# Experts that add their rows to per-token sums in DRAM, and logits taken from the narrow projection

## The chip, the cores and the metric

One core of a Trainium2 chip runs the whole kernel in one launch. The metric is device microseconds (us) from start to end, smaller is better. The engines are named as in the profile: PE (TensorE, matmuls), PEld (its weight loads), DVE (VectorE), ACT (ScalarE), POOL (GpSimd), SP (SyncE). SP, ACT and POOL each issue DMAs from a queue of their own. All numbers are float32.

## The reference, cut to what matters

```python
xn = layernorm(x)                                 # x: 8 sequences, 512 tokens, D = 256
out = x + attn(xn) * silu(ffn(xn))

def attn(x):                                      # 16 heads of 16
    q, k, v = silu(x @ Wq), l2_norm(silu(x @ Wk)), x @ Wv
    gk = log_sigmoid(x @ Wf1 @ Wf2)               # decay, by key
    a = k * -sigmoid(x @ Wgamma) * exp(gk)
    for t in range(512):                          # S: 16 x 16 for each head
        S = S * exp(gk[t])
        S = S + k[t] * (a[t] @ S + v[t])
        o[t] = q[t] @ S
    o = o * sigmoid(x @ Wog1 @ Wog2)
    return layernorm(o) * norm_w @ Wo

def ffn(x):                                       # 8 experts, each token takes 2
    w = softmax(x @ Wg + bg)
    top_w, top = top_k(w, 2);  cw = top_w / sum(top_w)
    out = sum(cw[e] * (gelu(x @ W1[e] + b1[e]) @ W2[e] + b2[e]) for e in top)
    return layernorm(out) * gamma + beta
```

## The kernel before

**Tiling.** The 4096 tokens are cut into eight stretches of 64 steps of all eight sequences (512 tokens, 4 tiles of 128 rows, `NP = 4`, `NT = 32` in all). Each stretch has four chunks of 16 steps, so the recurrence is a chain of 32 chunks.

**Prologue.** `load_tokens` loads x, half by SP's queue and half by ACT's. For every stretch `norm` normalizes in place, `transposed` (L208) turns the rows on PE, `logits` (L217) makes the gate's logits with 16 matmul records into the PSUM bank `pg`. Then `project(0)` runs: a narrow projection with `wfg_sb` (Wf1, Wgamma and Wog1 side by side, 80 columns), from which the decay is made with Wf2 (L258), then keys and queries (L231, L267) and values (L274). Results pass through the three buffers `stage` to DRAM; `spread` (L241) writes `kqd`. `gate` (L444 to L486) picks each token's two experts and their shares; inside it `route` (L300 to L431) counts the tokens of each expert, gives each of the 8192 token copies a row in `xs_dram` (`slot`), rounds the experts' ranges up to tiles of 256 rows (39 tiles, `NX`), finds the rows that stay free and the expert of each tile (`owner`). `scatter` (L493) writes the rows there: 64 indirect DMAs for two copies of 32 tiles, 14 with zeros for the free rows.

**Recurrence.** DVE prepares each stretch (`fine` and `solve`, L567 to L676). `fetch` and `turn_keys` (L515 to L529) load `kqd` and the gate g and turn them. Each chunk then takes `by_state` (L758, PE, which reads the state S), `sdec` (L767, POOL: S times its decay), `add_v` (L791, DVE, writes RO; POOL stores it to `ro`), `by_keys` (L825, PE) and `renew` (L837, DVE: the new S from PSUM and `sdec`). `output` (L888, L897, DVE) adds the part of the output inside a chunk; `attend` (L1032 to L1088) normalizes and projects a stretch and stores it in `att`.

**Experts.** `experts` runs over 39 tiles. SP loads the tile's rows (L933) and, at the address read from `owner` (L924), its expert's weights (L926, L928). PE makes h (L966), ACT applies gelu (L974). For each half n of a tile PE adds b2, picked by the one-hot `owned` (L986), and h times W2 (L994) in one PSUM bank; ACT copies both halves (L1004) and POOL stores them to `y_dram` (L950), in the order of `xs_dram`.

**Finish.** `gather` (L1098) fetches for each token tile its two rows of `y_dram` by `slot`: 64 indirect DMAs on POOL. `finish` scales one on ACT (L1113), adds the other with its share on DVE (L1117), normalizes, applies gamma, beta and silu, multiplies by `att` (L1146), adds x (L1148), which SP loads again (L1144), and stores (L1150, POOL).

**Order.** Every engine works through its instructions in a fixed order. The program is written out by three queues of generators, `inner` (recurrence's preparation), `between` (attention) and `beside` (everything else), which `stretch` spends credit on between the steps of the chain; a compile-time scheduler may move an instruction forward in front of others on its engine. `per_chunk` is the credit that `beside` gets in each chunk: projections of seven stretches and 39 expert tiles are spread over `PART` = 0.85 of the chunks.

## Time and profile before

| | |
|---|---|
| median of 9 runs | 1309.08 us (1292.92 to 1359.27) |
| profiled execution | 1306.15 us, its span 1304.4 us |
| mean granted PE clock | 0.852 |
| busy: PE, DVE, ACT, POOL | 979.4, 1070.3, 501.5, 413.0 us |
| DMA | 230.20 MB, mean 176 GB/s |
| renewals of the state (L837) | first at 236.6 us, last at 1196.1 us |
| last store to y_dram (L950) issued | 1054.8 us |

The profile comes from one execution. A busy engine isn't always the bound: what counts is which wait ends last in each stage, so the stages are read one by one: prologue (0 to 60), start of the chain with the projections (60 to 332), chain and experts together (332 to 1055), and the end (1055 to 1304).

### The profile page before, as it was taken

Reading aid. Unit: us, or ns where it says so; the run is one execution under the profiler, and the core shown is the slowest. Engines: PE = TensorE matmul, PEld = TensorE weight load, DVE = VectorE, ACT = ScalarE, POOL = GpSimd, SP = SyncE. Lnnn points to the kernel's source line nnn. Section 1 sums busy time; section 2 is a strip of 40 time slices with the busy share of each in tenths; the row PEclk is TensorE's granted clock in tenths of the full one; section 3 lists DMA queues with packets and bytes.
Section 4 is the critical chain, followed back from the end, with each engine's and each line's share of the span. In section 5 each row is a group of like instructions: output and inputs, shape, how many; then the busy total and the mean of one; then the engine's idle time right before and its main releaser. Section 6 shows DMA issues by size and latency. Waiting matters only on the chain.

```text
span 1304.4 us, 20560 instructions
## 1 busy us (share of the span) xinstructions
PE 979.4 (75%) x7679; PEld 738.4 (57%) x7679; DVE 1070.3 (82%) x2050; ACT 501.5 (38%) x814; POOL 413.0 (32%) x275
## 2 busy tenths in 40 slices
PE   5987657859999979999999899899998951310022
PEld 4743323438878768877787688678876830210021
DVE  5479675996999999999999998999999722768742
ACT  1375225435334234443442453344343212435222
POOL 0037781024115402511421141015111547782000
PEclk9998776879999979999999899889998975655566
DMA  8068575669768977796899589657947783463532
GB/s 173 1 175 205 154 225 108 158 184 280 216 191 257 152 193 241 232 204 167 264 167 250 150 283 213 168 166 259 205 133 218 141 172 114 126 187 86 97 80 64
DMA packets 389730, 230.20 MB, mean 176 GB/s; under 512 B 280024, under 2 KB 355904, under 8 KB 388608
## 3 DMA queue, kind: packets, MB, share of 16 engines
q1 hardware_dynamic: 368176, 176.99, 56.4%
q0 software_dynamic: 14672, 45.63, 11.2%
q10 hardware_dynamic: 6784, 6.29, 2.0%
q8 instruction: 60, 0.98, 0.3%
q14 instruction: 38, 0.31, 0.1%
HBM read 157.29 MB, written 71.57 MB: 175 GB/s over the span
## 4 chain that ended last, share of the span: by engine, by line
DVE 45%; DMA 14%; PE 13%; issue 11%; SPq 6%; ACT 5%; POOL 4%; ACTq 1%; DVEq 0%; POOLq 0%
DMA o<-O 5%; DVE Z L676 5%; DVE scratch_a L668 5%; DVE O L897 4%; DVE scratch_o L888 4%; DVE scratch_q L593 4%; DVE Z L610 4%; PE pp L231 3%; DVE scratch_a L593 3%; DVE Z L606 3%; DVE A L606 3%; DVE S L837 2%; POOL y L1098 2%; SPq L924 2%; PE pg L217 2%
## 5 line engine op out<-in xcount | busy, mean ns | idle before, releaser
L994 PE MATMUL py<-w,h 128*128 128x256 f32 x1248 | 307.0, 401 | 9.2 <-ACT h L974 9.2
L966 PE MATMUL ph<-xT_s,w 128*128 128x256 f32 x1248 | 289.5, 387 | 15.9 <-ACT sg L1057 7.2
L767 POOL TENSOR_TENSOR sdec<-S,PcF 128x1024 f32<-128x1024 f32 x31 | 181.6, 5858 | 367.1 <-DVE S L837 282.5
L994 PEld LDWEIGHTS py<-w,h 128*128 128x128 f32 x1248 | 240.7, 198 | 71.4 <-issue 24.8
L966 PEld LDWEIGHTS ph<-xT_s,w 128*128 128x128 f32 x1248 | 236.9, 193 | 52.5 <-ACT sg L1057 7.6
L974 ACT ACTIVATE h<-ph,bias 128x256 f32<-128x256 f32 x312 | 129.2, 473 | 116.3 <-PE ph L966 116.1
L668 DVE TENSOR_TENSOR scratch_a<-Z,A 128x1020 f32<-128x1020 f32 (+29 forms) x120 | 97.2, 810 | 15.5 <-ACT fq L632 15.4
L493 POOL DMA_INDIRECT xs_dram<-xn,slot x64 | 78.4, 1225 | 99.5 <-DVE which L406 80.3
L676 DVE TENSOR_TENSOR Z<-Z,scratch_a 128x1020 f32<-128x1020 f32 (+29 forms) x120 | 99.5, 830 | 0.2
L1004 ACT COPY y<-py 128x512 f32<-128x512 f32 x39 | 22.8, 584 | 185.7 <-PE py L994 185.7
L593 DVE TENSOR_TENSOR scratch_q<-Z,X 128x64 f32<-128x64 f32 (+15 forms) x128 | 93.3, 729 | 0.0
L606 DVE TENSOR_REDUCE Z<-scratch_q 128x4 f32<-128x64 f32 (+15 forms) x128 | 91.0, 711 | 0.0
L610 DVE TENSOR_TENSOR Z<-Z,X 128x64 f32<-128x64 f32 (+14 forms) x120 | 85.5, 712 | 0.0
L593 DVE TENSOR_TENSOR scratch_a<-Z,X 128x64 f32<-128x64 f32 (+14 forms) x120 | 84.6, 705 | 0.0
L606 DVE TENSOR_REDUCE A<-scratch_a 128x4 f32<-128x64 f32 (+14 forms) x120 | 81.0, 675 | 0.0
L950 POOL DMA_DIRECT2D y_dram<-y x39 | 28.7, 736 | 160.8 <-ACT y L1004 146.5
L1074 PE MATMUL pz<-ident,o_f 128*128 128x128 f32 x64 | 13.7, 340 | 85.9 <-ACT o_f L1028 71.0
L888 DVE TENSOR_TENSOR scratch_o<-Z,R 128x192 f32<-128x192 f32 (+22 forms) x120 | 72.4, 604 | 1.2 <-ACT fq L632 1.2
L897 DVE TENSOR_TENSOR O<-O,scratch_o 128x192 f32<-128x192 f32 (+22 forms) x120 | 73.0, 608 | 0.0
L825 PE MATMUL PC<-RO,KT 16*64 16x64 f32 x1984 | 34.6, 239 | 47.2 <-issue 22.2
L758 PE MATMUL PC<-S,FA 64*32 64x64 f32 x2048 | 31.5, 237 | 44.8 <-DVE S L837 41.1
L825 PEld LDWEIGHTS PC<-RO,KT 16*64 16x64 f32 x1984 | 28.1, 138 | 59.1 <-issue 27.5
(193 smaller groups left out, 1499.9 us busy)
## 6 DMA issues: line engine op xcount, KB each, us to landing
w<-in_L_ffn_W_dram SPq DMA_DIRECT2D x78, 1024.0 KB
kqd<-st_p SPq DMA_DIRECT2D x48, 256.0 KB
raw<-kqd SPq DMA_DIRECT2D x8, 1536.0 KB
xs<-xs_dram SPq DMA_DIRECT2D x39, 256.0 KB
y_dram<-y POOLq DMA_DIRECT2D x39, 256.0 KB
fq<-fq SPq DMA_DIRECT2D x8, 1024.0 KB
ro<-RO POOLq DMA_DIRECT2D x16, 512.0 KB
KT<-kt SPq DMA_DIRECT2D x132, 32.0 KB
```

The source lines that it names most:

```text
L493: ins = nc.gpsimd.indirect_dma_start(out=xs_dram[:, :], out_offset=bass.IndirectOffsetOnAxis(ap=to, axis=0), in_=what, in_offset=None,)
L593: nc.vector.tensor_tensor(pr, Z[:, :, :upto, C:], step[:, m, i].unsqueeze(2).to_broadcast([P, n, upto, HD]), ALU.mult,)
L606: nc.vector.tensor_reduce(to, pr, AX.X, ALU.add)
L610: nc.vector.tensor_tensor(Z[:, :, :i, C:], Z[:, :, :i, C:], step[:, 2, i].unsqueeze(2).to_broadcast([P, n, i, HD]), ALU.mult,)
L668: nc.vector.tensor_tensor(pr, Z[:, :, l, l:].unsqueeze(2).to_broadcast([P, n, l, w]), A[:, :, l, :l].unsqueeze(3).to_broadcast([P, n, l, w ...
L676: nc.vector.tensor_tensor(Z[:, :, :l, l:], Z[:, :, :l, l:], kept.pop(l), ALU.add)
L767: nc.gpsimd.tensor_tensor(dec.rearrange(flat), S.rearrange(flat), PcF[:, :, c].unsqueeze(2).to_broadcast([P, 16, SB]), ALU.mult,)
L888: nc.vector.tensor_tensor(pr, Z[:, :, j, j:C].unsqueeze(3).to_broadcast(shape), R[:, j].unsqueeze(2).to_broadcast(shape), ALU.mult,)
L897: nc.vector.tensor_tensor(o, o, kept.pop(j), ALU.add)
L966: nc.tensor.matmul(ph[:, k], w1[:, j, (f + k) * P : (f + k + 1) * P], xT[:, j], start=(j == 0), stop=(j == KD - 1),)
L974: nc.scalar.activation(h[:, k], ph[:, k], AF.Gelu, bias=bias[:, t, f + k : f + k + 1])
L994: nc.tensor.matmul(py[:, n], hs[f // 2][:, f % 2, n * P : (n + 1) * P], w2[:, f], start=False, stop=(f == NF - 1),)
```

## The change

1. **Sums in DRAM.** A scattered row becomes 258 wide: behind the 256 values stand the token's number and the share of that copy (`rows`, `DX`). `experts` scales each half tile by the share on ACT while it leaves PSUM, and an indirect DMA on POOL adds it to the token's row of `y_dram` (`add_to_sums`); rows of free places go to 128 spare rows. `start_sums` writes the shares' mix of b2 there first, so that the experts' bias matmuls go. In place of `gather`, `fetch_sums` loads whole tiles from SP.
2. **Logits.** `wfg_sb` gets Wg as columns 96 to 103; `narrow` runs this projection for every stretch in the prologue, transposes the logits back, and stores f1, og and the raw g in DRAM from ACT's queue. `project` loads f1 and makes the decay after keys and queries; g's sigmoid moves to `turn_keys`.
3. **x by the store.** SP copies x to out, DRAM to DRAM, and the last store adds to it.
4. Smaller: every other stretch's first half of x is loaded by POOL's queue, the weights of the narrow projection before them; `vz` is cleared by POOL at the start; `att_f` has three buffers, `xs` four; `per_chunk` reckons 12.8 for a projection, not 15.3.

```diff
...
-    xs_dram = dram.tile([NX * TS, D], F32, name="xs_dram")
-    y_dram = dram.tile([NX * TS, D], F32, name="y_dram")
+    DX = D + 2
+    xs_dram = dram.tile([NX * TS, DX], F32, name="xs_dram")
+    y_dram = dram.tile([NT * P + P, D], F32, name="y_dram")
...
+    rows = tokens.tile([P, NT, DX], F32, name="rows")
+    xn = rows[:, :, :D]
+    nc.gpsimd.iota(rows[:, :, D].bitcast(I32), [[P, NT]], base=0, channel_multiplier=1)
...
-        for bb, queue in enumerate((nc.sync, nc.scalar)):
+        for bb, queue in enumerate((nc.gpsimd if s % 2 else nc.sync, nc.scalar)):
...
+    b2_sb = gp.tile([P, 4, D], F32, name="b2_sb")
+    nc.gpsimd.memset(b2_sb, 0.0)
+    for q in range(4):
+        for n in range(4):
+            lo = 32 * q + E * n
+            nc.gpsimd.dma_start(b2_sb[lo : lo + E, n], b2)
...
+    def narrow(s, xT):
+
+        pfg = project_by(wfg_sb, xT, 0, FG)
+        gs = setup.tile([FG, B * NB], F32, name="gs", bufs=2)
+        nc.scalar.copy(gs, pfg[:FG])
         for n in range(NP):
-            for j in range(KD):
-                nc.tensor.matmul(
...
+            nc.tensor.transpose(
+                pg[:, (s * NP + n) * E : (s * NP + n + 1) * E],
+                gs[96:FG, n * P : (n + 1) * P],
+                ident[96:FG, 96:FG],
+            )
+        for lo, to in ((0, f1_d), (64, og_d)):
+            nc.scalar.dma_start(to[s], gs[lo : lo + HD])
+        nc.scalar.dma_start(
+            g_d[s].rearrange("(b h) t -> h b t", h=H),
+            gs[32 : 32 + H].rearrange("p (b t) -> p b t", b=B),
+        )
...
+    def start_sums(gp, cw):
+
+        nb = P // E
+        cwT = gp.tile([P, NT // nb, P], F32, name="cwT")
+        pc = bank("pc").rearrange("p (m t) -> p m t", t=P)
+        for m in range(NT // nb):
+            nc.tensor.transpose(
+                pc[:, m], cw[:, m * nb : (m + 1) * nb].rearrange("p n e -> p (n e)"), ident
+            )
+        nc.vector.tensor_copy(cwT, pc[:, : NT // nb])
+        for m in range(NT // nb):
+            for q in range(4):
+                at = slice(32 * q, 32 * q + 32)
+                for k in range(0, 4, 2):
+                    pb2 = bank("pb2")
+                    nc.tensor.matmul(
+                        pb2, cwT[at, m], b2_sb[at, k : k + 2].rearrange("p n d -> p (n d)"),
+                        start=True, stop=True,
+                    )
+                    st = setup.tile([P, B * NB], F32, tag="stage", name="st_b", bufs=3)
+                    nc.vector.tensor_copy(st, pb2)
+                    n = m * nb + 4 * q + k
+                    nc.sync.dma_start(
+                        y_dram[n * P : (n + 2) * P].rearrange("(n p) d -> p n d", p=P),
+                        st.rearrange("p (n d) -> p n d", n=2),
+                    )
...
+            nc.vector.tensor_copy(rows[:, :, D + 1], share[:, 0])
+            route(gp, wide, hot1, hot2, cw)
+            nc.vector.tensor_tensor(hot1, hot1, wide(share[:, 0]), ALU.mult)
+            nc.vector.tensor_tensor(hot2, hot2, wide(share[:, 1]), ALU.mult)
+            nc.vector.tensor_tensor(hot1, hot1, hot2, ALU.add)
+            start_sums(gp, hot1)
...
-        moves = [(slot[:, i, n : n + 1], xn[:, n]) for n in range(NT) for i in range(2)]
+        moves = [(slot[:, 0, n : n + 1], rows[:, n]) for n in range(NT)]
         moves += [(free[:, n : n + 1], zero) for n in range(free.shape[1])]
-        for to, what in moves:
+        moves += [(slot[:, 1, n : n + 1], rows[:, n]) for n in range(NT)]
+        for m, (to, what) in enumerate(moves):
+            if m == len(moves) - NT:
+                nc.gpsimd.tensor_copy(rows[:, :, D + 1], share[:, 1])
...
+        nc.scalar.activation(g, g, AF.Sigmoid)
...
-        def store(t, y):
-            nc.gpsimd.dma_start(
-                y_dram[t * TS : (t + 1) * TS].rearrange("(n p) d -> p n d", p=P), y
-            )
+        def add_to_sums(xs, n, y):
+            nc.gpsimd.indirect_dma_start(
+                out=y_dram[:, :],
+                out_offset=bass.IndirectOffsetOnAxis(
+                    ap=xs[:, n, D : D + 1].bitcast(I32), axis=0
+                ),
+                in_=y,
+                in_offset=None,
+                compute_op=ALU.add,
+            )
...
             for n in range(TS // P):
-                nc.tensor.matmul(
-                    py[:, n],
-                    owned[:E, t : t + 1].to_broadcast([E, P]),
-                    b2_sb,
-                    start=True,
-                    stop=False,
-                )
+                py = bank("py")[:, :D]
...
+                y = mp.tile([P, D], F32, name="y", bufs=4)
+                nc.scalar.activation(y, py, AF.Identity, scale=xs[:, n, D + 1 : DX])
+                add_to_sums(xs, n, y)
                 if n == 0:
                     yield 3.9
-            y = mp.tile([P, TS // P, D], F32, name="y")
-            nc.scalar.copy(y, py)
-            store(t, y)
...
+    def fetch_sums(fp, s):
+        g = fp.tile([P, NP, D], F32, name="g", bufs=NTB)
+        nc.sync.dma_start(
+            g,
+            y_dram[s * NP * P : (s + 1) * NP * P].rearrange("(n p) d -> p n d", p=P),
+        )
+        return g
...
-        nc.vector.tensor_tensor(xt, xt, g, ALU.add)
         for bb in range(2):
-            nc.gpsimd.dma_start(rows_of(out, s, bb), xt[bb * NB : (bb + 1) * NB])
...
+            nc.gpsimd.dma_start(
+                rows_of(out, s, bb), g[bb * NB : (bb + 1) * NB], accum_op=ALU.add
+            )
...
         projecting.close()
         prologue.close()
+
+        for b in range(B):
+            nc.sync.dma_start(out[b], x[b])
         with tc.tile_pool(name="moe", bufs=2, side="right") as mp:
             yield from experts(mp)
         fp = late.enter_context(tc.tile_pool(name="fin", bufs=2, side="right"))
-        ahead = {s: gather(fp, s) for s in range(2)}
+        sums = [fetch_sums(fp, s) for s in range(NTB)]
...
```

## The prediction

> **What bounds the kernel now.** First the page's slices (each digit is the busy share of 32.6 us in tenths):
>
> ```profile
> PE   5987657859999979999999899899998951310022
> DVE  5479675996999999999999998999999722768742
> POOL 0037781024115402511421141015111547782000
> PEclk9998776879999979999999899889998975655566
> ```
>
> Up to slice 32 VectorE (DVE) stands at 9 almost without a break, with TensorE (PE) beside it. In the last eight both fall, the granted PE clock drops to 0.5, and GpSimd (POOL) alone rises. The busy time by stage (us, then each engine with its count of instructions, the clock, the DMA share and GB/s) gives this in numbers:
>
> ```profile
> 0.00:60.00 60.00, 42.74 (x200) 39.65 (x200) 27.49 (x112) 13.52 (x28) 2.21 (x23) 1.00 0.45 94
> 60.00:140.00 80.00, 68.14 (x174) 32.75 (x175) 71.85 (x167) 49.31 (x64) 45.67 (x37) 0.87 0.64 169
> 140.00:250.00 110.00, 69.69 (x337) 33.85 (x336) 78.51 (x161) 43.32 (x56) 53.02 (x43) 0.72 0.65 162
> 250.00:332.00 82.00, 66.08 (x552) 47.27 (x551) 66.77 (x132) 38.50 (x53) 23.06 (x6) 0.88 0.85 234
> 332.00:700.00 368.00, 354.01 (x3064) 285.52 (x3063) 362.71 (x604) 145.21 (x254) 104.44 (x40) 0.97 0.82 208
> 700.00:1055.00 355.00, 334.07 (x2817) 267.63 (x2816) 327.38 (x524) 134.59 (x235) 83.30 (x38) 0.95 0.76 191
> 1055.00:1212.00 157.00, 28.05 (x488) 19.63 (x488) 94.28 (x231) 56.24 (x97) 97.24 (x83) 0.53 0.55 142
> 1212.00:1304.00 92.00, 16.64 (x56) 12.09 (x56) 41.26 (x123) 20.78 (x32) 4.02 (x6) 0.57 0.40 77
> ```
>
> From 332 to 1055 DVE works 690.1 of 723 us, PE 688.1: the recurrence's chain and the experts fill both, and only 33 us of DVE time are left. From 1055 to 1212, the experts being done, DVE works 94.3 of 157: 62.7 us of idling. The chain that ended last names POOL for this stage; its timeline (start, us, line, in brackets the idling before) shows why:
>
> ```profile
> 1060.24 1.03 POOL L1098 DMA_INDIRECT g<-y_dram,slot  x1 [4.68 <-DMA KT<-kt]
> ...
> 1099.74 0.96 POOL L1098 DMA_INDIRECT y<-y_dram,slot  x1 [0.30 <-issue]
> 1100.73 1.94 POOL L767 TENSOR_TENSOR sdec<-S,PcF 128x1024 f32<-128x1024 f32 x1
> ...
> 1178.47 0.96 POOL L1098 DMA_INDIRECT g<-y_dram,slot  x1 [0.30 <-issue]
> 1179.44 1.95 POOL L767 TENSOR_TENSOR sdec<-S,PcF 128x1024 f32<-128x1024 f32 x1
> ```
>
> POOL issues in order. The first gathers of `finish` (0.96 plus 0.30 us each) stand ahead of `sdec`, a link of the recurrence, which starts at 1100.73 although the state it multiplies was renewed at 1055.03; the renewals after that are at 1129 (its last part), 1164 and 1195, where before they came 27 to 35 us apart with the experts in between. The waits tell who else stood by:
>
> ```profile
> ACT g L1113 <- DMA g<-y_dram,slot: 43.6, 15, 6.4
> DVE g L1117 <- ACT g L1113: 23.7, 6, 9.6
> DVE g L1117 <- DMA y<-y_dram,slot: 15.9, 4, 6.7
> POOL sdec L767 <- DVE S L837: 282.5, 20, 35.5
> ```
>
> The stage's idling is gathers: POOL issuing them, then ACT and DVE waiting for their landing. The last 92 us (1212 to 1304) are another thing, the serial way from the last chunk through `R`, `output`, `attend(7)` and the last `finish`.
>
> **The change, part by part.** The sum is made against the profiled execution, 1306.15 us (span 1304.4), 2.9 under the median of 1309.08.
>
> *End of the kernel, 1055 to 1212.* 64 gathers go (48.8 + 32.4 us of POOL and 64 gaps of 0.30: 100 us), so do 32 scalings on ACT (15.5) and 32 L1117 on DVE (17.2), and six of the eight L1148 (6 x 1.2 = 7.2) fall in this stage. DVE's work here becomes 94.3 - 17.2 - 7.2 = 69.9. In their place eight `fetch_sums` of 512 KB go out from SP. They can't start before the last add has landed: 1.3 us of issue, 3.4 to 6.9 of landing (gathers: issued 1060.24 and in use at 1063.65; issued 1174.65 and in use at 1181.6), then some 5 for the first load (`xs`, 256 KB, ended waits of 4.6 and 4.9). So `finish` starts some 11 us in, while three chunks of recurrence still run. Of the 62.7 us of idling I keep half (32: this start, the ACT to DVE handings to and fro, key loads queued behind 4 MB of sums on SP). The stage is then 102 us, **55 saved**. Bounds: all idling stays, 24 saved; none stays, 87.
>
> *The last 92 us.* Two L1148 go (2.4), the x loads too; the output's store becomes an add. It is issued at 1296.50 and the execution ends 8 us later; an add that takes one more gather's landing costs up to 3.4. I take **0**, bounds -2.4 and +3.4.
>
> *Experts, 332 to 1055.* Gone: 156 bias matmul records (L986, 56.9 us of PE) and 39 stores (L950, 28.7 us of POOL). Added: ACT takes 78 x 0.50 instead of 39 x 0.584, +16 us, hidden by ACT's 280 of 723. POOL gets 78 indirect adds at about 1.0 + 0.3 = 1.3 each (101 us; it works 188 of 723 here). The new wait matters: two adds may meet in one row of y_dram, and unlike the scatter they are not declared independent, so each waits on POOL until the one before has landed, and behind it in the queue stand `sdec`, then through `renew` DVE, and the stores of `ro` and `att`. An add comes every (1054.9 - 311.9)/78 = 9.5 us, so POOL keeps up while a landing takes less than 9.5 - 1.3 = 8.2 us; `sdec` has a chunk of some 30 us to run in, needs 5.9 (L767's mean), and three adds of 8 still fit. The trace has no accumulating DMA. Its nearest rows are the gathers, 3.4 to 6.9 us at a DMA share of 0.55, here it is 0.79. I expect 6 to 8, just below the point: some late `sdec`, which eat what less PE work gives back. I take **0**; bounds -33 (all DVE idling goes with the 56.9) and +140 (a landing of 10 us: 78 x 1.8).
>
> On this wait the Trainium skill speaks twice. Its page "DMA: Bandwidth & Descriptors", under "Rules for kernel authors", says that an accumulating DMA reads its destination and writes it later, and that another write in between is lost, so one must wait for the earlier DMA's semaphore: the rule makes the serial wait unavoidable, and it speaks against this change. The same page, "Anatomy of one DMA — SWDGE (gpsimd) path", gives 2.0 us plus bytes over 436 KB per us; for 128 KB that is 2.3 us, an estimate by which an add would hold POOL 3.6 us, be never late, and leave the sum at 1261 or, with the 33, at 1228; by the gathers' landings it is 1261 too, by a landing of 10 it is 1400. No run here shows which holds for an add.
>
> *Prologue, 0 to 60.* A stretch holds PE for eight transposes (1.95) and sixteen records of L217 (3.64). The narrow projection does it in four records (1.92 at 60.07) and four small transposes (by L208, 0.22 each: 0.9): 0.8 less, eight times 6.6. After the last one a copy (0.6) and the transposes come on top, 1.5. **-5**; if PE waits out the copy each time (0.6 + 0.3), +2. The three stores per stretch go to ACT's queue (v's took 0.63 each, 15 us in all), which works 13.5 of 60 here.
>
> *Start, 60 to 332.* Removed per stretch: the projection (now earlier), the L249 sigmoid with its table load (1.28), two SP issues. Added: 16 sums of b2 by PE (K = 32, by L258 0.76 a record), 16 copies on DVE (by L791, 0.68: 10.9), four products and copies (1.5), 16 stores of 256 KB, all through the three `stage` buffers that `project` uses; SP also loads f1 (eight times 0.35) in place of those two issues, and the sigmoid comes back once per stretch in `turn_keys`, on an ACT that works 131 of 272 here. **+12**, DVE's 12.4 put on the path. If the 14.4 us that DVE waits at 152 to 166 (for `fq` on ACT) cover it, 0; if the copies wait for buffers as ACT's L267 did (45.3 us), +45. The value loads and constants of later code were issued far ahead (L924 from 83 on, L1158 at 23), so I put the eight 512 KB copies of x to out into 20 to 60, where DMA is 0.18 busy, at no cost; beside the first weights at 285 (share 1.00, 291 GB/s in 290 to 332) 8.4 MB would cost up to 29. On POOL the b2 loads, x loads and memsets lie before 83, where it is idle; in `scatter` the second share's copy waits for the landing of what was issued before it, one landing of up to 6.9, with 32 scatters and the first `sdec` (201.0) behind it. That `sdec` is done 34 us before the first renewal at 236.65: 0; without that cover, 7.
>
> Sum: -55 + 0 + 0 - 5 + 12 = -48: 1258 on the profiled execution, **1261** on the median's scale.
>
> **Rivals.** *POOL becomes the bound* (slower). One mechanism: the landing of an add under the experts' traffic, deciding from 8.2 us on, 78 us for each us above; 9 us cancel the gain (1261 + 62 = 1323), 10 give 1400. For it: DMA at 0.79 and `o<-O` landings of 12 to 18 us on the chain. Against: gathers at 3.4 to 6.9, and sdec's slack. *The start eats it*: buffers +33 over my value and the copies of x +29 give 1323; for it the 45 us of ACT waits on `kqd`, against it that kqd of stretch 1 is only loaded at 184. *The end stays idle*: the gathers were hiding other latencies (key loads, handings), 24 saved instead of 55: 1292. *Gathers only changed into adds*, which is what the diff does by count (64 to 78 indirect DMAs): then POOL's work stays, but it is spread over 743 us in which POOL is idle for 70%, so the end is still relieved; this would have to appear as the first rival. *More than forecast*: idling goes wholly and PE's relief reaches DVE: 1261 - 32 - 20 = 1209.
>
> **How the numbers follow.** Forecast (1235 to 1285) 0.45, more than forecast 0.14, end stays idle (1285 to 1322) 0.18, POOL the bound 0.15, start eats it 0.08. One per cent, about what a measurement of this kernel can tell from no change, is 1296 and 1322: faster is 0.45 + 0.14 and half of 0.18, 0.68; the other half, and a little of the slower two, 0.11 within; 0.21 slower. The range cuts some 0.07 below and 0.13 above: 1205 to 1345; the forecast's own is 1235 to 1285.
>
> **What would show it.** Right: `sdec` within 5 us of its renewal after the experts' end, that stage about 100 us, 332 to 1055 about as long as before, first renewal of the chain some 5 to 10 us later than 236.6. Wrong: long POOL waits for the add's own landing with `sdec` late behind them; DVE waits for `stage` buffers before 250; or idling of 60 us after the experts with no gather in it.

## The result, and the profile after

The changed kernel is slower: 1339.06 us median (1332.59 to 1341.41, 10 runs) against 1303.65 us of the kernel before, 1.0269 times as long, 95% interval 1.0241 to 1.0297. The forecast was 1261. In two more sets further down it is 1.0152 and 1.0316. The profiled execution took 1332.76 us, its span 1331.1, 26.7 over the span before. (One run further down, `nosums`, took 1283 to 1325 us and was profiled in an execution of 1325, so no time is taken from that profile.)

The slices of the page again, now 33.3 us each:

```profile
PE   2853339686898985998889897986789579411221
DVE  4474368999499996999699889987998699599652
POOL 4057750301333551354234432732274035403001
PEclk9965659788899896998889998997889789655666
```

Three things differ from before. DVE has a hole in the fourth to sixth slice (4, 3, 6; before 9, 6, 7); from the eleventh to the 35th ten of its 25 slices lie under nine, at 4 to 8. The end is shorter. By stage, cut at the marks that answer to those of before (first and last add, in place of first and last store to y_dram; us, then PE, PEld, DVE, ACT and POOL with their counts, clock, DMA share, GB/s):

```profile
60.00:140.00 80.00, 36.88 (x85) 17.94 (x85) 47.69 (x132) 17.51 (x19) 47.67 (x43) 0.60 0.59 183
140.00:250.00 110.00, 64.24 (x218) 31.68 (x219) 76.59 (x124) 36.69 (x47) 46.44 (x37) 0.72 0.57 152
250.00:354.00 104.00, 78.22 (x613) 49.64 (x613) 94.17 (x182) 41.73 (x60) 18.08 (x6) 0.79 0.72 173
354.00:700.00 346.00, 297.84 (x2555) 250.42 (x2554) 304.77 (x510) 144.68 (x250) 130.77 (x52) 0.92 0.85 197
700.00:1154.00 454.00, 374.00 (x3387) 314.64 (x3385) 401.84 (x660) 179.51 (x314) 185.20 (x67) 0.90 0.79 184
1154.00:1239.00 85.00, 8.71 (x387) 7.08 (x388) 72.11 (x190) 38.04 (x61) 19.64 (x16) 0.50 0.72 145
1239.00:1331.00 92.00, 24.45 (x87) 17.74 (x86) 37.48 (x120) 19.51 (x32) 8.67 (x10) 0.61 0.56 97
```

DVE works 124 of the 190 us from 60 to 250, where before it worked 150; and 706.6 of 800 from the first add to the last, where before it worked 703.6 of 742.9 from first store to last. In the last 177 us it works 110.

From these marks the 26.7 us add up (to rounding):

| part | before | after | difference | forecast |
|---|---|---|---|---|
| gate: `scatter` starts | 83.2 | 79.4 | -4 | -5 |
| start: from there to the first y store or add | 228.8 | 274.8 | +46 | +12 |
| experts: first to last y store or add | 742.9 | 799.9 | +57 | 0 |
| end: last y store or add to the end | 249.6 | 176.9 | -73 | -55 |

The end gave more than was forecast. The start and the experts took it all back, and 27 more. The start's 46 us lie ahead of the first renewal: from `scatter` to the second `sdec` it takes 202.7 us where it took 155.2, from there to the first add 72.1 where it was 73.5 to the first store.

### The profile page after: what moved, and what is told of

Its sections match the earlier page's. It is cut to its first block, busy times and chain, and to the rows that moved or that the text cites. A ratio compares the mean times of both kernels' runs of the same rounds, so it can differ in the third digit from the quotient of the medians.

```text
span 1331.1 us, 20257 instructions
## 1 busy us (share of the span) xinstructions
PE 913.6 (69%) x7461; PEld 705.3 (53%) x7461; DVE 1061.8 (80%) x2027; ACT 498.8 (37%) x819; POOL 472.5 (36%) x275
## 5 line engine op out<-in xcount | busy, mean ns | idle before, releaser
L998 POOL DMA_INDIRECT y_dram<-y,xs x78 | 214.6, 2752 | 386.1 <-ACT y L1050 186.8
L1021 PE MATMUL ph<-xT_s,w 128*128 128x256 f32 x1248 | 298.2, 395 | 39.8 <-ACT sg L1105 28.7
L1042 PE MATMUL py<-w,h 128*128 128x256 f32 x1248 | 298.0, 396 | 18.7 <-ACT h L1029 18.7
L1021 PEld LDWEIGHTS ph<-xT_s,w 128*128 128x128 f32 x1248 | 243.4, 198 | 78.5 <-ACT sg L1105 29.5
L815 POOL TENSOR_TENSOR sdec<-S,PcF 128x1024 f32<-128x1024 f32 x31 | 130.0, 4194 | 231.4 <-DVE S L885 125.8
L1050 ACT ACTIVATE y<-py,xs 128x256 f32<-128x256 f32 x78 | 36.8, 472 | 183.6 <-PE py L1042 183.6
L646 DVE TENSOR_TENSOR scratch_a<-Z,X 128x64 f32<-128x64 f32 (+14 forms) x120 | 88.4, 737 | 14.1 <-issue 7.0
L545 POOL DMA_INDIRECT xs_dram<-rows,slot x64 | 70.0, 1094 | 73.4 <-DVE which L428 54.2
L945 DVE TENSOR_TENSOR O<-O,scratch_o 128x192 f32<-128x192 f32 (+22 forms) x120 | 76.9, 641 | 0.0
L1096 DVE TENSOR_TENSOR o_f<-o_f,by_state 128x1024 f32<-128x1024 f32 x8 | 9.8, 1226 | 77.4 <-DMA KT<-kt 28.7
L1122 PE MATMUL pz<-ident,o_f 128*128 128x128 f32 x64 | 15.3, 381 | 78.6 <-ACT o_f L1076 78.6
```

What stands on the lines that cost most here:

```text
L646: nc.vector.tensor_tensor(pr, Z[:, :, :upto, C:], step[:, m, i].unsqueeze(2).to_broadcast([P, n, upto, HD]), ALU.mult,)
L815: nc.gpsimd.tensor_tensor(dec.rearrange(flat), S.rearrange(flat), PcF[:, :, c].unsqueeze(2).to_broadcast([P, 16, SB]), ALU.mult,)
L945: nc.vector.tensor_tensor(o, o, kept.pop(j), ALU.add)
L998: nc.gpsimd.indirect_dma_start(out=y_dram[:, :], out_offset=bass.IndirectOffsetOnAxis(ap=xs[:, n, D : D + 1].bitcast(I32), axis=0), in_=y, ...
L1021: nc.tensor.matmul(ph[:, k], w1[:, j, (f + k) * P : (f + k + 1) * P], xT[:, j], start=(j == 0), stop=(j == KD - 1),)
L1042: nc.tensor.matmul(py, hs[f // 2][:, f % 2, n * P : (n + 1) * P], w2[:, f], start=(f == 0), stop=(f == NF - 1),)
```

## The experiments

Ratios are to the kernel before on the same chip; which chip a set of runs gets is not chosen, and the kernel before took some 1273 us on some and 1298 to 1308 on others, so its time stands beside each. "Second sdec" is when `sdec` starts for the second time, at the end of the first renewal of the state (before 238.4, after 282.1). "Experts" is first to last add or store.

| run | ratio, 95% interval | us, beside before's | second sdec | experts | end |
|---|---|---|---|---|---|
| ids | 1.0044, 1.0012 to 1.0075 | 1301.3, 1298.4 | 280.8 | 767.8 | 178.9 |
| dx272 | 1.0330, 1.0238 to 1.0421 | 1342.5, 1298.4 | 281.3 | 811.5 | 179.5 |
| ownst | 1.0308, 1.0223 to 1.0392 | 1338.0, 1298.4 | 279.8 | 807.4 | 178.7 |
| nosums | 0.9977, 0.9923 to 1.0031 | 1299.1, 1298.4 | see the text | | |
| w256 | 0.9806, 0.9764 to 0.9847 | 1248.1, 1273.2 | 227.7 | 769.7 | 179.0 |
| b258 | 1.0020, 0.9998 to 1.0042 | 1276.2, 1273.2 | 221.6 | 746.4 | 235.5 |
| alt | 1.0127, 1.0057 to 1.0196 | 1288.9, 1273.2 | 232.8 | 809.5 | 179.2 |
| best1 | 0.9716, 0.9674 to 0.9759 | 1237.3, 1273.2 | 221.7 | 758.8 | 175.3 |
| after2 | 1.0152, 1.0113 to 1.0192 | 1326.9, 1307.8 | 281.9 | 801.9 | 177.9 |
| before2 | 0.9990, 0.9961 to 1.0019 | 1306.3, 1307.8 | 242.4 | 745.4 | 250.0 |
| plain | 0.9868, 0.9836 to 0.9900 | 1288.3, 1307.8 | 282.6 | 746.6 | 184.8 |
| best1_2 | 0.9499, 0.9464 to 0.9533 | 1239.0, 1307.8 | 229.7 | 755.3 | 175.1 |
| paced | 1.0305, 1.0254 to 1.0357 | 1312.5, 1274.0 | 250.2 | 810.5 | 179.2 |
| ids_paced | 0.9998, 0.9976 to 1.0019 | 1273.0, 1274.0 | 249.1 | 767.4 | 180.8 |
| best1_b2 | 0.9719, 0.9668 to 0.9769 | 1239.1, 1274.0 | 227.3 | 759.1 | 176.3 |
| nosums2 | 1.0043, 1.0019 to 1.0068 | 1279.2, 1274.0 | 221.0 | 806.3 | 179.7 |
| after3 | 1.0316, 1.0231 to 1.0401 | 1340.3, 1298.6 | 282.1 | 807.2 | 177.5 |
| best1_nox | 0.9449, 0.9379 to 0.9520 | 1226.3, 1298.6 | 222.2 | 764.9 | 185.2 |

### The experts: who waits for an add

The prediction looked at POOL's queue. What SP's own queue waited for in the changed kernel, from 354 to 1154 (line, releaser: us in all, times, longest):

```profile
SPq L981 <- DMA y_dram<-y,xs: 146.4, 22, 15.3
SPq L976 <- PE py L1042: 70.3, 18, 7.9
SPq L776 <- DVE RO L839: 38.7, 6, 15.1
```

L981 is `load_rows`. It stands 146 us until an add has landed, because an add reads its list of token numbers out of the buffer `xs` itself, so the buffer comes free only then, and with four buffers the load of the rows four tiles later wants it. Before, the same load waited 49 us, for PE's transposes:

```profile
SPq L933 <- PE pt L942: 48.7, 15, 6.9
```

Behind it in SP's queue stand the loads of keys, of og and o, of `raw`, and the weights. DVE, which idled for 39 us in this stage before and 93 now, shows who is late:

```profile
DVE o_f L1096 <- DMA KT<-kt: 26.8, 2, 15.1
DVE dec L626 <- ACT X L579: 19.3, 1, 19.3
DVE o_f L1096 <- DMA xs<-xs_dram: 12.6, 1, 12.6
DVE o_f L1096 <- DMA og<-og: 10.8, 1, 10.8
DVE scratch_a L721 <- ACT fq L685: 9.1, 4, 3.1
DVE o_f L1096 <- DMA o_f<-o: 7.4, 1, 7.4
```

**ids** takes this one reason away:

```diff
+            own = mp.tile([P, TS // P], I32, name="own", bufs=4)
+            nc.gpsimd.tensor_copy(own, xs[:, :, D].bitcast(I32))
...
-                    ap=xs[:, n, D : D + 1].bitcast(I32), axis=0
+                    ap=own[:, n : n + 1], axis=0
```

> The changed kernel with one thing taken away: an add no longer reads the token numbers out of the buffer of rows (xs) but from a small copy that POOL makes, so the buffer comes free when PE and ACT are done with it, not when the add has landed. Theory (SP): the 57 us that the experts' stage lost (743 to 800 us from its first to its last store or add) are SP standing 146 us at the next load of rows, with the loads of keys, og, o and raw behind it, for which DVE waits some 75 us. Then SP's waits for landed adds fall under 30 us, the stage comes to 745 to 765, the time to 1285 to 1305. Rival (POOL, the step of the prediction): the adds' own waits on POOL hold sdec back. Then the stage stays at 785 to 800 and the time at 1325 to 1345.

Measured: 1301.3 us, and the experts' stage 767.8. Of SP's waits for landed adds one is left, 10.1 us at the first load of the finished sums. The list is led by the load of W2, which waits for PE to be done with its buffer, as in the kernel before (78.4 us there):

```profile
SPq L976 <- PE py L1044: 123.8, 25, 11.8
```

So 32 of the 57 us, and 38 of the kernel's time, were the buffer that an add holds. The changed kernel itself did not run beside `ids`. Beside dx272 and ownst of the same set, which hold the buffer, it is 40 to 44 us of the stage and 37 to 41 of the time. Two pairs further down say the same: freeing the buffer takes 41 us between alt and w256 (which differ in the row length and the scatter's order too) and 40 between paced and ids_paced. The rival as it was written is refuted. The stage came out 3 us above the theory's span, so something is left over.

**plain** takes the adds away altogether:

```diff
-            nc.gpsimd.indirect_dma_start(
-                out=y_dram[:, :],
...
-                compute_op=ALU.add,
-            )
+            at = t * TS + n * P
+            nc.gpsimd.dma_start(y_rows[at : at + P], y)
```

> The changed kernel with 78 plain stores of the scaled half tiles, each to rows of its own in DRAM, in place of the adds: the sums keep b2's mix alone. Nothing waits for the landing of the one before, nothing reads the numbers out of the buffer of rows. Theory: the adds cost the experts' stage all it lost; then it takes 740 to 752 us from the first store to the last and the time is 50 to 60 under the changed kernel's. The small copy of the numbers gave 32 us of stage and 38 of time, so some 20 would be the adds' serial landing on POOL. Rival (those 20 are other things: ACT's half copies, per_chunk, loads): 760 to 772, 35 to 42 under.

Measured: 1288.3 us, 38.6 under the changed kernel beside it (after2), and a stage of 746.6. The stage is where the theory put it; the time is not, it gained 39 by the medians (47 by the profiled spans) where 50 to 60 were expected, which lies in the rival's span: from the last store on it takes 185 us where the changed kernel takes 177 to 178. One line each from first to last add or store, in the order before, changed kernel, ids, plain:

```profile
311.90:1054.80 742.90, 707.98 (x6074) 569.31 (x6072) 703.60 (x1166) 295.92 (x508) 189.61 (x80) 0.96 0.80 201
```

```profile
354.20:1154.10 799.90, 671.63 (x5939) 564.89 (x5937) 706.61 (x1169) 324.19 (x563) 315.95 (x118) 0.91 0.82 190
```

```profile
352.50:1120.20 767.70, 673.40 (x5937) 566.19 (x5935) 704.27 (x1169) 324.57 (x563) 336.69 (x154) 0.92 0.83 198
```

```profile
354.20:1100.80 746.60, 663.97 (x5868) 559.31 (x5866) 696.36 (x1148) 324.44 (x563) 171.51 (x119) 0.93 0.78 202
```

DVE's work hardly differs (third pair: 704, 707, 704, 696 us); its idling is 39, 93, 63 and 50. POOL's busy time is 172 with plain stores and 316 or 337 with adds. What `ids` leaves against `plain`, 21 us of the stage, is what the adds cost on POOL, their longer issue and their waits together: 13 us are idling of DVE, and 8 are work of DVE that `plain` does after the last store (1148 instructions in the stage for 1169). In the kernel's time the two are 13 us apart, on two chips. On POOL the wait for the add before is now in the open:

```profile
POOL y_dram L998 <- DMA y_dram<-y,own: 97.3, 22, 7.4
...
POOL own L1040 <- DMA y_dram<-y,own: 35.6, 9, 6.3
```

When an add waits for the one before it, the two start 7.0 us apart in `ids` and 8.0 in the changed kernel (medians; the least spacing of any two is 4.6 and 4.8), and from the end of the issue to the next start it is 2.9 to 8.1. Below the 9.5 us at which one comes, then, but with `sdec`, stores and copies queued among them.

### The start: beats of 0.7 us

The hole in DVE's row has a shape that no wait in the prediction has. The timeline of the changed kernel (start, us; in brackets the idling before):

```profile
141.55 0.58 ACT L235 COPY xT<-pt 128x512 f32<-128x512 f32 x1 [38.02 <-remote]
142.95 0.48 DVE L646 TENSOR_TENSOR scratch_a<-Z,X 128x256 f32<-128x256 f32 x1 [2.07 <-issue]
144.35 0.49 DVE L646 TENSOR_TENSOR scratch_q<-Z,X 128x320 f32<-128x320 f32 x1 [0.92 <-issue]
145.75 0.42 DVE L659 TENSOR_REDUCE A<-scratch_a 128x16 f32<-128x256 f32 x1 [0.91 <-DVE scratch_q L646]
146.45 0.49 DVE L663 TENSOR_TENSOR Z<-Z,X 128x320 f32<-128x320 f32 x1 [0.28 <-DVE A L659]
147.28 0.97 POOL L545 DMA_INDIRECT xs_dram<-rows,slot  x1 [0.30 <-issue]
148.55 0.97 POOL L545 DMA_INDIRECT xs_dram<-rows,slot  x1 [0.30 <-issue]
```

From 135 to 180 us many of DVE's starts are 0.70, 1.40 or 2.10 us apart, although each of these operations takes 0.4 to 0.8 and needs only earlier ones of DVE. ACT's copy at 141.55 waits for nothing but PE's transposes; in after2, the same kernel's second profile, these end at 115.1 and 120.7 and ACT's two copies start at 139.8 and 151.0. Updates of semaphores (by which one engine tells another that it is done) are recorded 13 to 18 times in each 10 us from 100 to 190, where they come 62 to 178 times from 60 to 100 and 65 to 298 times from 200 to 320. Only POOL keeps its pace: a scatter each 1.27 us. The kernel before shows a thinner form of it, 22 to 66 updates from 130 to 180. From 100 to 140 us, in the order before, changed kernel, alt:

```profile
100.00:140.00 40.00, 33.01 (x78) 14.57 (x77) 40.00 (x77) 21.53 (x30) 31.32 (x28) 0.83 0.68 182
```

```profile
100.00:140.00 40.00, 12.06 (x22) 4.66 (x20) 17.47 (x43) 0.26 (x1) 30.72 (x31) 0.50 0.56 187
```

```profile
100.00:140.00 40.00, 37.05 (x94) 17.87 (x94) 38.34 (x84) 13.18 (x20) 31.45 (x29) 0.80 0.90 259
```

DVE works 40.0, 17.5 and 38.3 of these 40 us.

**dx272** pads the rows:

```diff
-    DX = D + 2
+    DX = D + 16
...
+    nc.gpsimd.memset(rows[:, :, D + 2 :], 0.0)
```

> The changed kernel with scattered rows of 272 values (1088 bytes, a multiple of 64) in place of 258 (1032 bytes); f1 shares a buffer with gs to make room. Theory (rows): the start lost 45 us because from 102 to 190 us, beside the scatter, DVE, ACT, PE and SP get on only in beats of 0.7 us, and the odd row length does that. Then the beats go, the second sdec starts at 240 to 255 in place of 282.1, and the time is 1300 to 1315. Rival (beats have another cause, or none of the loss): second sdec at 277 to 287, time 1332 to 1345.

Measured: second sdec at 281.3, the beats unchanged. That the length isn't a multiple of 64 bytes is out as the cause.

**ownst** gives `start_sums` buffers of its own:

```diff
-                    st = setup.tile([P, B * NB], F32, tag="stage", name="st_b", bufs=3)
+                    st = gp.tile([P, B * NB], F32, name="st_b", bufs=4)
```

> The changed kernel with four buffers of its own for start_sums in place of the three that it shares with the projections. Theory (buffers, the bound of the prediction): the projection of stretch 1 was pushed from 80-98 us to 142-197 because the sums hold the buffers. Then it runs by 120 us, the second sdec starts at 240 to 260 in place of 282.1 and the time is 1300 to 1318. Rival (rows or scatter): the beats of 0.7 us stay, the projection still ends after 180, second sdec at 275 to 285, time 1330 to 1345.

Measured: 279.8, beats unchanged. So the bound of the prediction that came true in size (+45) did not come true in kind: the shared buffers cost some 2 us at most.

**nosums** starts from zeros:

```diff
+    nc.sync.dma_start(
+        y_dram[: NT * P].rearrange("(n p) d -> p n d", p=P),
+        zero[:, :D].unsqueeze(1).to_broadcast([P, NT, D]),
+    )
...
-            start_sums(gp, hot1)
```

> The changed kernel without start_sums: the sums start from zeros, written by one early DMA of 4 MB from SP, and b2 is left out of the result. It takes away 16 matmul pairs, 16 copies on DVE and 16 stores of 256 KB between 90 and 132 us. If start_sums (its work or its buffers) is the cause of the start's 45 us, the second sdec starts at 238 to 250 and the time is 1290 to 1305. If the scatter alone is, the beats of 0.7 us stay from 102 to 190, second sdec at 265 to 282, time 1320 to 1340.

Measured: 1299.1 us, 39 to 43 under ownst and dx272 of the same set, about the whole loss of the start. Where in the kernel they were saved isn't shown. Its profile has the long row of beats, 13 to 17 updates in each 10 us from 110 to 190, with the second sdec at 265.2; so it is not shown that the beats need start_sums.

**w256**, **b258** and **alt** came on a chip where the kernel before takes 1273 us. w256:

```diff
-    xs_dram = dram.tile([NX * TS, DX], F32, name="xs_dram")
+    xs_dram = dram.tile([NX * TS, D], F32, name="xs_dram")
...
-        moves = [(slot[:, 0, n : n + 1], rows[:, n]) for n in range(NT)]
+        moves = [(slot[:, 0, n : n + 1], xn[:, n]) for n in range(NT)]
```

> The changed kernel with scattered rows of 256 values as before, so without the token number and the share in them: the adds take made-up token numbers (still different in each of the 128 rows) and made-up shares, so the sums are other ones; an add then also doesn't hold the buffer of rows. Theory (row length): rows of more than 1024 bytes make the beats of 0.7 us beside the scatter. Then DVE is busy over 80% from 100 to 140 us as before (it is 44% in the changed kernel), the second sdec starts at 240 to 262, and with the buffers freed early the time is 1265 to 1285. Rival (length is nothing): beats stay, second sdec at 275 to 285, time 1295 to 1305, as with the small copy of the numbers.

b258, the kernel before with long rows:

```diff
-    xs_dram = dram.tile([NX * TS, D], F32, name="xs_dram")
+    xs_dram = dram.tile([NX * TS, D + 2], F32, name="xs_dram")
...
-    xn = tokens.tile([P, NT, D], F32, name="xn")
+    rows = tokens.tile([P, NT, D + 2], F32, name="rows")
+    xn = rows[:, :, :D]
```

> The kernel before with rows of 258 values in the scatter and the loads of rows, nothing else: the mirror of the last one. Theory (row length): DVE falls under 60% busy from 100 to 140 us (it is 100% there), second sdec from 238 to 265 or later, time up by 20 to 45 us. Rival: second sdec within 4 us of 238, time within 1%.

alt:

```diff
-        moves = [(slot[:, 0, n : n + 1], rows[:, n]) for n in range(NT)]
+        moves = [(slot[:, i, n : n + 1], rows[:, n]) for n in range(NT) for i in range(2)]
         moves += [(free[:, n : n + 1], zero) for n in range(free.shape[1])]
-        moves += [(slot[:, 1, n : n + 1], rows[:, n]) for n in range(NT)]
...
-            if m == len(moves) - NT:
-                nc.gpsimd.tensor_copy(rows[:, :, D + 1], share[:, 1])
```

> The changed kernel with the scatter in the order of before (both copies of a tile in turn, then the zeros) and without the copy of the second shares on POOL, so the second copy carries the first one's share. Theory (order: runs of 32 scatters from neighbouring rows, zeros in the middle, cause the beats): beats gone, second sdec at 240 to 262, time 1300 to 1320. Rival (order is nothing): second sdec at 277 to 287, time 1330 to 1345.

None of the three shows beats (96 to 318 updates in each 10 us from 100 to 190). Taken alone, w256 and alt would have seemed to confirm two different theories, although both came out below the times these gave (1248 for 1265 to 1285, 1289 for 1300 to 1320). b258, the mirror of w256, shows no loss at all with the long rows (1.0020), and its second sdec is at 221.6, where its rival had 234 to 242 and the theory 265 or later: a sign that the place differed, not the edit. Neither change of the changed kernel was run where there are beats, so what the order and the length have to do with them is untested.

**after2** and **before2** are the two kernels unaltered, in one set with plain and best1_2:

> The changed kernel itself, unaltered, beside the runs that follow. The other order of the scatter and the rows of 256 values both showed no beats of 0.7 us, but so did the kernel before with rows of 258, and its own times were 2% lower there. Theory (place): the beats belong to the chip that a run is on, not to an edit; then the changed kernel shows them or not together with the other kernels of this set: without them second sdec at 228 to 240 and 1.010 to 1.018 times the kernel before, with them 275 to 287 and 1.024 to 1.035. Rival (order or row length makes them): beats here, with second sdec at 275 to 287, while the kernel before shows DVE over 95% busy from 100 to 140 us and updates of semaphores over 100 in 10 us from 130 to 170.

> The kernel before itself, for its profile beside those of this set: with beats its semaphore updates fall to some 25 in 10 us from 130 to 170 and the second sdec starts at about 238; without them over 100, and the second sdec at 218 to 225.

Both came on a chip where the kernel before takes 1308, and both show beats: after2 from 100 to 190, second sdec at 281.9, though its ratio, 1.0152, is below the 1.024 to 1.035 expected with them; before2 22 to 23 updates in 10 us at 140 and at 170, second sdec at 242.4. The kernel before loses to them too: from the start of the scatter to the second sdec it takes 155 and 154 us (before, before2), and 133 in b258, with the same 123 to 124 us of DVE's work in it. That is 21 to 23 of the some 30 us between its times on the two kinds of chip.

**after3**, in the last set:

> The changed kernel itself once more. If the kernel before takes some 1273 us beside it, the theory (beats belong to the chip, and lengthen what the edit costs) expects no beats, second sdec at 229 to 237 (221 without start_sums, 233 with the other order of the scatter), the experts' stage still 800 to 812, and 1.010 to 1.020 times the kernel before; the rival (the edit makes them everywhere) 14 updates in 10 us from 100 to 190 and 1.030 to 1.045. If the kernel before takes 1300 or more: beats, second sdec at 281 to 283, 1.015 to 1.030.

Again a chip of 1299, and beats, second sdec at 282.1, ratio 1.0316. So the changed kernel itself was never profiled where the kernel before takes 1273. What stands: no kernel profiled there (w256, b258, alt, best1, paced, ids_paced, best1_b2, nosums2) shows the long row of beats; on the others every version with start_sums does (second sdec 280 to 283), and nosums in its one profile. In the place without beats start_sums can be priced: **nosums2** against alt.

> The changed kernel without start_sums once more (b2 left out), for the profile of an undisturbed execution. If start_sums carries most of the start's loss by its work on PE, DVE and SP: second sdec at 225 to 245, and no beats or short ones. If it is the stream alone: beats from 102 to 190 and second sdec at 262 to 270, as in the first profile.

Measured: no beats, and the second sdec at 221.0, 4 us earlier than its theory had it; with start_sums it is 232.8 in alt and 227.7 in w256. That is 7 to 12 us, where the prediction had put 12.

**paced** and **ids_paced** were to test what makes the beats:

```diff
+            one = slot[:, 0, :1].to_broadcast([P, 200])
+            nc.gpsimd.tensor_tensor(pace, one, one, ALU.add)
```

> The changed kernel with an idle operation of POOL (200 elements, some 0.4 us) after each of the 78 indirect DMAs of the scatter; nothing else. Theory (stream): the scatter's unbroken row of issues, one each 1.27 us, holds back the other engines' semaphore updates. Spaced to 1.65 or more, updates stay over 60 in 10 us from 110 to 180, DVE is busy over 80% from 110 to 140 (35% in the changed kernel), the scatter ends some 30 us later (218), yet the second sdec starts at 230 to 262 in place of 282, and the time is 20 to 50 us under the changed kernel's. Rival (the issues are nothing): updates stay at 14, second sdec at 282 or later by what the scatter is longer, time the same or up to 30 us over.

> The same pacing together with the small copy of the token numbers: by the stream theory 38 us less than the paced run, 0.945 to 0.985 of the kernel before; by the rival 0.995 to 1.02 of it.

They came on a chip without beats, where there is nothing to take away: the scatter ended at 245 instead of some 205, sdec waited for it, and paced took 1.0305. So the stream theory was not tested. It stays open what starts the beats. They were seen only beside the scatter, and only on chips where the kernel before takes 1298 us or more. There the long row came in every profile of a kernel that has start_sums or the 16 small loads of its b2 on POOL's queue (nosums keeps these). It did not come in those that have neither: the kernel before, and best1_2 and best1_nox further down.

### Versions that beat both

**best1** puts together what the two halves taught: the copy of the numbers, sums from zeros, and b2 again by the one-hot matmul of the kernel before:

```diff
+                nc.tensor.matmul(
+                    py, owned[:E, t : t + 1].to_broadcast([E, P]), b2_own, start=True, stop=False
+                )
```

> The changed kernel with the token numbers copied out of the buffer of rows, and the sums started from zeros by one early DMA, b2 being added by the experts' one-hot matmul as in the kernel before (78 records). If the two gains add (38 us for the copy, 40 for the sums), the time is 1260 to 1275 and below before; if the bias matmuls, 57 us of PE, come on the path of the experts' stage, 1280 to 1310.

> The version with the small copy of the token numbers and sums that start from zeros, once more, beside the changed kernel: 0.965 to 0.98 of the kernel before, and 45 to 75 us under the changed kernel.

Measured: 1237.3 and 1239.0, 0.9716 of the kernel before on the one chip and 0.9499 on the other, 88 us under the changed kernel beside it. That is more than the two gains added, in both expectations by 13 to 23 us; where the rest comes from was not taken apart. The version's own time hardly knows the chip; what differs is the kernel before. On the chip with beats its second sdec is at 229.7 (updates fall to 16 to 20 only from 190 to 210). No cost of the 78 bias matmuls shows: the experts' stage takes 755 to 759, less than with `ids` alone.

**best1_b2** put the unused loads of b2 back:

```diff
+    b2_sb = gp.tile([P, 4, D], F32, name="b2_sb")
+    nc.gpsimd.memset(b2_sb, 0.0)
...
+            nc.gpsimd.dma_start(b2_sb[lo : lo + E, n], b2)
```

> The best version so far with the 16 loads of b2 on POOL's queue and their clearing put back, unused. If these bring the beats: updates under 25 in 10 us from 110 to 180, second sdec from 222-230 to 260 or later, time up by 25 to 45 us over the best version's 0.95 to 0.97 of the kernel before. If they are nothing: 0.945 to 0.975, second sdec at 220 to 232.

1239.1, second sdec 227.3: no cost in time shows, but this too was a chip without beats, so whether they matter for those isn't told.

**best1_nox** undoes part 3 in best1:

```diff
-        for b in range(B):
-            nc.sync.dma_start(out[b], x[b])
...
+            nc.sync.dma_start(xt[bb * NB : (bb + 1) * NB], rows_of(x, s, bb))
...
+        nc.vector.tensor_tensor(xt, xt, g, ALU.add)
```

> The best version with part 3 undone: no copies of x to out, x is loaded and added on DVE in the last step (eight additions of 1.2 us) and the last store is plain. By the prediction's terms (2.4 us of the last stage, some 7 of the one before, the copies free): the tail from the last add grows from 175 to 178-186 us and the time by 3 to 10 us. Rival (8.4 MB of copies cost the start something): the second sdec 3 to 10 us earlier and the time the same or lower.

The fastest: 1226.3 us, 0.9449 of the kernel before. The first add comes at 275.4 where best1 has it at 300.8 and 306.6, while the second sdec stands at 222.2 against 221.7 and 229.7; the end takes 185.2 instead of 175. So the end does what the theory said (178 to 186), the time does what the rival said, but the gain comes behind the second sdec, where neither had it. Of the eight copies best1 issues four after 100 us (106.6, 122.5, 186.5 and 239.9). The last goes out 36 us ahead of the experts' first load of rows (276.3; 251.6 without the copies), and between them stand stores of the last projection, whose very last comes 25 us later than without the copies (273.8 against 249.0). Which way the copies hold this back, in SP's queue, in the traffic or in the order of the instructions, was not taken apart. Part 3 gives the end its 10 us and puts off the start of the experts by 25 to 31; without it their stage is 6 to 10 us longer, and 11 to 13 us are the net price. best1 was not run beside it; the two versions are compared across chips (1237.3 and 1239.0 against 1226.3).

## Why the prediction was wrong

**What bounds the kernel, and the end: right.** The gathers were the stage's idling. After the last add `sdec` starts 6.0 us or less behind its renewal, where it was 44, 17 and 13 late:

```profile
1154.12 1.56 POOL L998 DMA_INDIRECT y_dram<-y,xs  x1 [5.37 <-DMA y_dram<-y,xs]
1155.12 2.52 POOL L815 TENSOR_TENSOR sdec<-S,PcF 128x1024 f32<-128x1024 f32 x1
1189.75 1.93 POOL L815 TENSOR_TENSOR sdec<-S,PcF 128x1024 f32<-128x1024 f32 x1 [32.10 <-DVE r L1072]
1198.02 2.77 POOL L815 TENSOR_TENSOR sdec<-S,PcF 128x1024 f32<-128x1024 f32 x1 [3.75 <-DVE S L885]
```

The saving is 73 where 55 was forecast: I kept half of the idling, 32 us; from 1154 to 1239 DVE works 72.1 of 85 (forecast 69.9), so 13 stayed. The rival "the end stays idle" is refuted.

**Prologue: right in size** (-4 for -5; between before2 and after2 it is -9). What gave it was not taken apart.

**Experts: the failed step.** The sum put 0 there, on the ground that POOL keeps up while a landing takes less than 8.2 us. The landings were about as taken (a waiting add starts 2.9 to 8.1 us after the end of the issue before it), only the issue cost more, 2.0 us by the median where 1.0 was taken from the gathers; by the median the point was not crossed (8.0 us from one start to the next where 9.5 are to be had; 5 of the 17 adds that waited took longer), and `sdec` was late only now and then: seven of the 24 in the stage started 5 to 14 us after the renewal they need, and each still ended 8.6 us or more before the next one. So the rival "POOL becomes the bound" did not happen in its own way either. What failed is the search for who is queued behind the add. I named POOL's queue and forgot the operand: the index list lies in `xs`, the add holds `xs` until it lands, `load_rows` waits for `xs`, and SP's queue, with the loads for DVE behind it, waits for `load_rows`. The diff shows it in one line (`ap=xs[:, n, D : D + 1]`), and its `bufs=4` in place of 2 hints that the buffer is held longer; I read it as a detail. It costs 32 us of the stage and 38 of the time (ids), by the other pairs up to 44 and 41; 21 more of the stage, 13 of them DVE's idling, are the adds on POOL (plain).

On the two statements of the Trainium skill weighed in the prediction ("DMA: Bandwidth & Descriptors"): the rule under "Rules for kernel authors", that an accumulating DMA must wait for the earlier one's semaphore, rightly warned of a cost: POOL waits 97.3 us for landed adds in `ids`. That a sum would be lost without the wait, no run here shows. The formula under "Anatomy of one DMA — SWDGE (gpsimd) path" gave an estimate of 2.3 us. In best1, whose trace has the landing of 68 of its 78 adds, it comes 2.1 to 7.8 us after the end of the issue, 4.4 by the median, beside the experts' traffic. So the estimate is that of the quickest adds; the measurement decides.

**Start: a second step that failed; the term was about right for its reason and missed another.** +12 was put for start_sums; where there are no beats it costs 7 to 12 (nosums2 against w256 and alt). Where there are, the start is 46 longer, and the reason is none that the prediction weighed: the buffers (its bound) are refuted by ownst, and what makes the beats stays open. The trace of before had the sign in it, SP advancing by 0.7 us beside the scatter. The path was held even then: DVE's wait of 14.4 us for `fq`, which the prediction offered as cover, is 0.9 us in b258, on a chip without beats. That the copies of x cost nothing, since they would go out by 60 us, was wrong too: the profile has them at 25.9 to 72.0, 197.0, 212.5 and 283.4, and with them in best1 the first add comes 25 to 31 us later than without, about the 29 that stood as the bound. What they cost in the changed kernel itself was not run.

**The signs named.** Right, nearly: sdec after the experts (at most 6.0 us late, forecast 5), and that stage (85 us, forecast 102). Wrong: 332 to 1055 got longer; the first renewal is 44 us later, not 5 to 10. Of the signs of failure, "long POOL waits for the add's own landing" appear (69 us), but the deciding one, SP's wait at L981, was not on the list.

## What to carry to other kernels

For every operand of an asynchronous instruction, its index list too, ask until when the buffer is held and which queue next wants that buffer: a small copy of the list was worth 38 us here. A transfer that nothing waits for (a copy from DRAM to DRAM) need not be free: here the next stage came 25 to 31 us later with it, and the version without it was 11 to 13 us faster. Compare a version with its parent on one chip, and before believing that an edit cured something, see that the sickness is there in an unaltered kernel beside it.

## What was not expected of the hardware

Beside a run of indirect DMAs from POOL, one each 1.27 us, semaphore updates of all other engines can fall to one in some 0.7 us (13 to 18 recorded in 10 us), with an update 25 us late; DVE then works 17.5 of 40 us. It appears for some 90 us in the changed kernel and thinner in the kernel before, on chips where the latter takes 1298 to 1308 us, and was not seen where it takes 1273. Its cause is open. An add of 128 rows of 1 KB to DRAM holds POOL 2.0 us by the median, and up to 12.2 (a gather of as many rows 0.96 by the median).
